# Last attention's keys of five tiles begun while the second layer's pipeline fills, its values while the third layer's pipeline empties

## The chip, the cores and the metric

The kernel runs on one core of a Trainium2 chip. A core has five engines with an instruction stream each: TensorE (PE: matrix products and transposes, into PSUM), VectorE (DVE), ScalarE (ACT), GpSimd (POOL) and SyncE (SP, which issues the DMAs here). Each stream runs in its written order; semaphores make one engine wait for another. The metric is the device time of one execution in microseconds (us), the median of the runs, lower being better.

## The reference

Four layers are applied to x, 16 sequences of 128 tokens with 256 features; a second input, ctx, has the same shape. Each layer is a cross-attention to ctx and a feed-forward part, both with a layer norm ahead and added to x. Cut to what matters, with numpy-like names:

```python
for xattn, ffn in layers:                 # layers 0, 1, 2, 3
    x = x + xattn(layernorm(x), ctx)
    x = x + ffn(layernorm(x))

def L3_xattn(x, cond):                    # the last attention: all tokens of all sequences
    q = x @ Wq + bq                       # 16 heads of 16
    k, v = split(cond @ Wkv + bkv)        # of ctx alone, not of x
    q, k = fake_int8(q, per token and head), fake_int8(k, per token and head)
    v = fake_int8(v, scale over all 2048 tokens)
    p = fake_uint8(softmax(q @ k.T))
    return (p @ v) @ Wp + bp
```

Layers 0 to 2 attend within a sequence, so a tile of 128 tokens passes through them by itself. The last attention has every token attend to all 2048 context tokens, so that all keys and values have to be there before its first tile is done. Its keys and values depend on ctx alone, so they can be worked out at any time before. The scale of the values is a maximum over all tokens: the values are computed once for the maximum and once more to be quantized.

## The kernel before

The work falls into three sections. `l0` does layer 0; `middle` does layers 1 and 2 and, beside them, the keys and values of layer 3; `l3` does layer 3. A tile is one sequence (128 tokens on the partitions); x stays in SBUF in 16 tiles for the whole kernel.

In `middle` each piece of work is a Python generator, and a `yield` ends a step of it. `side_by_side` (L122) takes a table that says at which step each generator starts, and advances all running generators by one step in turn. This gives the order in which instructions are recorded. Outside `l3`, whose order is written out by hand, the framework's scheduler then lays the recorded instructions out on each engine. The table before: tile t begins the second layer's attention (`l1_xattn`) at step 4t, its feed-forward part (`l1_ffn`) at 4t+3, the third layer's attention (`l2_xattn`, eight steps) at 4t+7, its feed-forward part (`l2_ffn`, four steps) at 4t+16, and the last attention's keys of tile t (`l3_keys`, three steps) at 4t+2. The values (`l3_values`, 17 steps) begin at step 4. So a tile enters every four steps; steps 0 to 16 fill the pipeline, and from step 64 on it empties, the last step being 79.

PSUM has eight banks, shared out by tag: e (1 bank: all of `l1_xattn`, and transposes and the last product of `l1_ffn`), w (3: the wide products of both feed-forward parts), x (2: `l2_xattn`), av (1), and f (1: transposes and the last product of `l2_ffn`, and in the version before all of the keys and values). The stream of keys and values, "kv", has one buffer for each SBUF tile that it names.

One piece of values (`piece`, L836) is a product of two 128x512 float32 matmuls into a bank (vT), and an ACT copy with the bias into SBUF (L841). In the first eight steps DVE then takes the maximum (L845). In the later eight, DVE scales and rounds (L853), POOL subtracts the rounding constant into a bfloat16 tile vi (L855), PE transposes its four blocks (vtp, L859), and ACT copies them into `v_int` (L860). One tile of keys is a product of two 128x256 matmuls in a bank (k), its quantization on DVE and POOL (from L773 and L818), a split into three bfloat16 parts on DVE (L824, L826), and eight transposes (htp, L789) with an ACT copy (L790).

What leaves each stage is added to x on DVE: line 608 after `l1_xattn`, 675 after `l1_ffn`, 717 after `l2_xattn`, 770 after `l2_ffn`. In `l2_ffn` the products vecs are followed by a routing on DVE, POOL's z (L764), z's transposes and the product out. When the middle is over, its SBUF is given to the weights of `l3`.

Of the kernel before, what the change touches and what calls it, by code (L numbers as in the profile page):

```python
# [30 lines left out]
NT = 16  # L31
# [9 lines left out]
class Net:  # L41
# [820 lines left out]
    def middle(self, w3):  # L862

        with (self.tc.tile_pool(name="w1", bufs=1) as self.w, self.psum(e=1, w=3, x=2, av=1, f=1)):
            self.tag = "e"
            w1f = self.l1_ffn_weights()
            w2x, w2f, w3k = self.l2_xattn_weights(), self.l2_ffn_weights(), self.l3_kv_weights()
            with (self.stream("f", bufs=1, small=2) as s2f, self.stream("x", bufs=1, small=2) as s2x,
                  self.stream("kv", bufs=1, small=2, tag="f") as s3, self.stream("f1", bufs=1, small=2, tag="e") as s1f,
                  self.stream("x1", bufs=1, small=2, tag="e") as s1x):  # L870
                starts = {}
                for t in range(NT):
                    for step, st, make in ((0, s1x, lambda p, t=t: self.l1_xattn(t, p)),
                                           (3, s1f, lambda p, t=t: self.l1_ffn(t, w1f, p)),
                                           (7, s2x, lambda p, t=t: self.l2_xattn(t, w2x, p)),
                                           (16, s2f, lambda p, t=t: self.l2_ffn(t, w2f, p)),
                                           (2, s3, lambda p, t=t: self.l3_keys(t, w3k, w3, p))):
                        starts.setdefault(4 * t + step, []).append((st, make))
                starts[4].append((s3, lambda p: self.l3_values(w3k, w3, p)))
                self.side_by_side(starts)  # L880
        self.tag, self.small = None, self.small0

# [379 lines left out]
```

## Time and profile before

| what | value |
|---|---|
| median of three runs | 3008.33 us (3003.62 to 3014.27) |
| time of the profiled execution | 3011.51 us |
| span of its instructions | 3009.8 us |
| PE busy | 2460.5 us (82%) |
| DVE busy | 1956.3 us (65%) |
| ACT busy | 1755.0 us (58%) |
| POOL busy | 1000.7 us (33%) |
| first and last exit of line 608 | 1183.3 and 1736.7 us |
| first and last exit of line 770 | 1329.7 and 1862.5 us |

A profile is of one execution; its instants are us from the span's start. A line of a timeline has the start, the duration, the engine, the source line, the operation, the tile written and those read, the shape, the number of instructions merged, and in brackets the idle time of the engine just before it and who ended that. A line of a tile has the smallest, median and largest duration in ns, and the first and last start. A line of waits has the sum, the number and the longest, in us. A float32 matmul shows as two records. The granted clock is the share of full speed that TensorE was allowed.

### The profile page before, as it was taken

Reading aid. Unit: us, or ns where it says so; the run is one execution under the profiler, and the core shown is the slowest. Engines: PE = TensorE matmul, PEld = TensorE weight load, DVE = VectorE, ACT = ScalarE, POOL = GpSimd, SP = SyncE. Lnnn points to the kernel's source line nnn. Section 1 sums busy time; section 2 is a strip of 40 time slices with the busy share of each in tenths; the row PEclk is TensorE's granted clock in tenths of the full one; section 3 lists DMA queues with packets and bytes.
Section 4 is the critical chain, followed back from the end, with each engine's and each line's share of the span. In section 5 each row is a group of like instructions: output and inputs, shape, how many; then the busy total and the mean of one; then the engine's idle time right before and its main releaser. Section 6 shows DMA issues by size and latency. Waiting matters only on the chain. (4 is left out here: it accounts for less than half of the span.)

```text
span 3009.8 us, 41685 instructions
## 1 busy us (share of the span) xinstructions
PE 2460.5 (82%) x14066; PEld 1556.2 (52%) x14066; DVE 1956.3 (65%) x5041; ACT 1755.0 (58%) x4636; POOL 1000.7 (33%) x1587
## 2 busy tenths in 40 slices
PE   4789999999999875888888885777777777777778
PEld 2456666666666543456555653344444444444445
DVE  2455666666665434566666653887788787878784
ACT  1234444444444332555555541998888888888885
POOL 2344444444443322555555541111111111112111
PEclk9899999999999887999999997589899898989999
DMA  5000000000000003000000002876666666666673
GB/s 205 1 1 1 1 1 1 1 1 1 1 1 1 1 28 102 6 3 5 5 5 4 3 1 72 154 135 123 124 117 128 121 124 121 126 122 125 118 128 62
DMA packets 559830, 171.38 MB, mean 57 GB/s; under 512 B 538912, under 2 KB 555904, under 8 KB 558848
## 3 DMA queue, kind: packets, MB, share of 16 engines
q1 hardware_dynamic: 559616, 168.72, 27.8%
q8 instruction: 111, 1.82, 0.2%
q14 instruction: 103, 0.84, 0.1%
HBM read 32.37 MB, written 2.10 MB: 11 GB/s over the span
## 5 line engine op out<-in xcount | busy, mean ns | idle before, releaser
L938 ACT ACTIVATE p<-piece,nb,hs 128x512 int16<-128x512 f32 x1024 | 785.2, 791 | 27.4 <-issue 17.0
L922 DVE TENSOR_REDUCE nm<-piece 128x1 f32<-128x512 f32 x1024 | 652.1, 684 | 107.7 <-PE piece L916 99.8
L916 PE MATMUL piece<-kst,qT 128*128 128x512 bf16 x1024 | 366.5, 414 | 200.6 <-DVE ma L1099 89.6
L1100 POOL TENSOR_TENSOR act<-ma,mb 128x176 f32<-128x176 f32 x160 | 89.0, 558 | 765.1 <-DVE ma L1099 764.7
L233 PE MATMUL gu<-w_L_ffn_wgu,mhT 128*128 128x352 f32 x640 | 252.5, 523 | 11.6 <-ACT p L938 8.0
L225 ACT COPY pT<-tp 128x512 f32<-128x512 f32 (+1 forms) x208 | 116.6, 563 | 201.6 <-PE tp L209 200.1
L916 PEld LDWEIGHTS <-qT 128*128 128x128 bf16 x1024 | 77.4, 99 | 297.2 <-issue 168.8
L938 ACT ACTIVATION_READ_ACCUMULATOR p<-piece,nb,hs 128x1 f32 x1024 | 222.2, 217 | 0.0
L259 POOL TENSOR_TENSOR kx<-kT,hmask 128x512 f32<-128x512 f32 x128 | 132.8, 1043 | 190.4 <-PE scores L262 125.4
L264 DVE TENSOR_REDUCE mx<-scores 128x4 f32<-128x512 f32 x128 | 88.2, 689 | 161.3 <-PE scores L262 161.0
L233 PEld LDWEIGHTS gu<-w_L_ffn_wgu,mhT 128*128 128x128 f32 x640 | 122.7, 205 | 131.4 <-ACT p L938 83.5
L950 PEld LDWEIGHTS <-pT 128*128 128x128 f16 x4096 | 144.7, 99 | 82.6 <-issue 68.0
L278 PEld LDWEIGHTS av<-v,pT 128*128 128x128 f32 x1024 | 136.2, 201 | 78.2 <-ACT pT L225 66.6
L233 PE MATMUL gu<-w_L_ffn_wgu,hT 128*128 128x352 f32 x512 | 173.7, 461 | 2.1 <-DVE act L432 1.6
L524 ACT ACTIVATE s<-s,nb,qs 128x128 f32<-128x128 f32 x256 | 123.2, 482 | 87.2 <-DVE nb L522 87.2
L278 PE MATMUL av<-v,pT 128*128 128x17 f32 x1024 | 136.3, 265 | 41.0 <-ACT pT L225 41.0
L269 ACT ACTIVATE p<-scores,mx,qs 128x128 f32<-128x128 f32 x256 | 96.9, 459 | 118.8 <-DVE mx L267 111.0
L950 PE MATMUL av<-v_int,pT 128*128 128x16 bf16 x4096 | 143.7, 171 | 19.6 <-DVE o L1021 19.6
L262 PE MATMUL scores<-kx,qT 128*128 128x512 f32 x256 | 153.0, 682 | 2.3 <-ACT qT L225 1.8
L539 PE MATMUL oproj<-w_L_ffn_oT,oT 128*128 128x256 f32 x512 | 128.9, 396 | 3.7 <-ACT oT L533 3.6
L1119 PE MATMUL moe<-w_L_ffn_wd,aT 128*128 128x256 f32 x448 | 127.7, 434 | 3.6 <-ACT p L938 3.6
L233 PE MATMUL q<-w_L_ffn_qT,hT 128*128 128x512 f32 x256 | 127.9, 600 | 2.1 <-DVE rot L478 2.0
(362 smaller groups left out, 5305.7 us busy)
## 6 DMA issues: line engine op xcount, KB each, us to landing
pT<-p SPq DMA_TRANSPOSE x256, 4.3
w_L_ffn_wgu<-in_L_ffn_wgu SPq DMA_DIRECT2D x1, 3520.0 KB, 11.6
w_L_ffn_wgu<-in_L_ffn_wgu SPq DMA_DIRECT2D x1, 2816.0 KB, 12.7
x<-in_x SPq DMA_DIRECT2D x16, 128.0 KB, 4.5
ctxT<-in_ctxT SPq DMA_DIRECT2D x4, 512.0 KB, 5.2
w_L_ffn_qT<-in_L_ffn_qT SPq DMA_DIRECT2D x1, 2048.0 KB, 7.9
w_L_ffn_oT<-in_L_ffn_oT SPq DMA_DIRECT2D x1, 2048.0 KB, 15.6
ctx<-in_ctx SPq DMA_DIRECT2D x16, 128.0 KB, 2.0
```

The costliest lines, as they stand in the source:

```text
L225: nc.scalar.copy(out[:, j0:j0 + m, :], ps)
L233: self.nc.tensor.matmul(ps, a, b, start=(j == 0), stop=(j == n - 1))
L259: nc.gpsimd.tensor_tensor(kx, kT[oc].unsqueeze(1).to_broadcast([P, 4, P]), self.hmask[:, hs].unsqueeze(2).to_broadcast([P, 4, P]), ALU.mult)
L262: nc.tensor.matmul(ps, qT[:, oc, :], kx, start=True, stop=True)
L278: nc.tensor.matmul(av[:, 4 * g + h, :], pT[:, h, :], v[:, 4 * g + h, :], start=True, stop=True)
L524: nc.scalar.activation(s[:, j, :], s[:, j, :], AF.Exp, bias=nb[:, j:j + 1], scale=qs[:, j:j + 1], accum_out=z[:, j:j + 1])
L539: nc.tensor.matmul(proj, oT[:, j, :], w["o"][:, c, :], start=(c == 0), stop=(c == 15))
L916: nc.tensor.matmul(ps, qTs[t % 2][:, hd, :], kst[q // 2][:, hd // 2, 512 * (q % 2):512 * (q % 2) + 512], start=True, stop=True)
L922: nc.vector.tensor_reduce(st["nm", u][:, q:q + 1], st["s", u, q][0], AX.X, ALU.max, negate=True)
L938: nc.scalar.activation(p[:, 512 * q:512 * q + 512], ps, AF.Exp, bias=nb, scale=st["sq", t][:, hd:hd + 1], accum_out=st["z", t][:, hd, q:q ...
L950: nc.tensor.matmul(st["av", t][:, hd, :], pb[:, c, :], v[:, c, hd * 16:(hd + 1) * 16], start=(c == 0), stop=(c == NT - 1))
L1119: nc.tensor.matmul(ps, st["aT", k][:r, j, :], wd[:r, c, :], start=(c == 0), stop=(c == 13))
```

## The change

The keys leave the table of the loop over tiles. A loop of its own starts them at step 2t for the first five tiles (0, 2, 4, 6, 8) and at 4t-8 from the sixth on (12, 16, ..., 52). The values begin at step 61 instead of step 4, and take their PSUM from bank e instead of bank f. Keys stay in bank f. No instruction is added or removed.

```diff
-                                           (16, s2f, lambda p, t=t: self.l2_ffn(t, w2f, p)),
-                                           (2, s3, lambda p, t=t: self.l3_keys(t, w3k, w3, p))):
+                                           (16, s2f, lambda p, t=t: self.l2_ffn(t, w2f, p))):
                         starts.setdefault(4 * t + step, []).append((st, make))
-                starts[4].append((s3, lambda p: self.l3_values(w3k, w3, p)))
+
+
+                for t in range(NT):
+                    starts.setdefault(2 * t if t < 5 else 4 * t - 8, []).append((s3, lambda p, t=t: self.l3_keys(t, w3k, w3, p)))
+                starts.setdefault(4 * NT - 3, []).append((s3[:2] + ("e",), lambda p: self.l3_values(w3k, w3, p)))
                 self.side_by_side(starts)
```

## The prediction

> **What bounds the kernel now.** The page's slices first: the middle section, which the change touches, is slices 15 to 24 of the 40.
>
> ```profile
> span 3009.8 us, 41685 instructions
> ...
> PE   4789999999999875888888885777777777777778
> ...
> PEclk9899999999999887999999997589899898989999
> ```
>
> PE is the fullest engine in the middle and no other comes near it. Next, busy time by stage of that section. Columns: stretch, its length, then busy us of PE, PEld, DVE, ACT and POOL, granted clock, DMA share, GB/s.
>
> ```profile
> 1183.00:1330.00 147.00, 117.72 (x510) 69.36 (x510) 86.26 (x257) 74.46 (x175) 80.04 (x123) 0.89 0.02 6
> 1330.00:1745.00 415.00, 357.46 (x1779) 246.50 (x1777) 283.29 (x797) 222.94 (x567) 219.85 (x353) 0.94 0.01 4
> 1745.00:1820.00 75.00, 62.90 (x305) 42.82 (x304) 36.73 (x87) 35.33 (x87) 24.26 (x35) 0.93 0.00 1
> 1820.00:1862.50 42.50, 20.56 (x66) 13.93 (x66) 13.26 (x27) 3.91 (x7) 9.63 (x10) 0.72 0.00 0
> ```
>
> The rows are the fill, the steady part, and the emptying in two pieces. PE is 80% busy in the fill, 86% when the pipeline is full (one tile each 37.5 us), 84% in the first part of the emptying and 48% in its last 42 us. Then the tile that moves, and what its instructions wait for:
>
> ```profile
> L233 PE MATMUL vT<-ctxT,w_L_xattn_Wkv x64: 592/592/1223, 1190.1 to 1314.5; 128*128 128x512 f32 x64
> L841 ACT ACTIVATE vT<-vT,c_L_xattn_bkv x16: 687/688/720, 1196.5 to 1315.5; 128x512 f32<-128x512 f32 x16
> L845 DVE TENSOR_REDUCE vam<-vT x8: 670/680/686, 1197.2 to 1236.6; 128x1 f32<-128x512 f32 x8
> L853 DVE TENSOR_SCALAR vT<-vT,vr x8: 476/486/781, 1243.5 to 1319.4; 128x512 f32<-128x512 f32 x8
> L855 POOL TENSOR_SCALAR vi<-vT x8: 1499/1505/1595, 1244.3 to 1321.2; 128x512 bf16<-128x512 f32 x8
> ...
> PE vtp L859 <- POOL vi L855: 7.5, 5, 3.0
> ```
>
> All values work lies in the fill. Last, the emptying in order of time: where each of the last five tiles leaves (line 770), and PE and POOL around the last two.
>
> ```profile
> 1744.96 0.41 DVE L770 TENSOR_TENSOR x<-out,x 128x256 f32<-128x256 f32 x1
> 1779.47 0.42 DVE L770 TENSOR_TENSOR x<-out,x 128x256 f32<-128x256 f32 x1 [1.04 <-PE out L233]
> 1811.27 0.42 DVE L770 TENSOR_TENSOR x<-out,x 128x256 f32<-128x256 f32 x1 [3.73 <-PE out L233]
> 1838.70 0.42 DVE L770 TENSOR_TENSOR x<-out,x 128x256 f32<-128x256 f32 x1 [12.23 <-PE out L233]
> 1862.54 0.42 DVE L770 TENSOR_TENSOR x<-out,x 128x256 f32<-128x256 f32 x1 [11.83 <-PE out L233]
> ```
>
> ```profile
> 1814.10 3.68 PE L233 MATMUL vecs<-w_L_ffn_AT,hT 128*128 128x512 f32 x8
> ...
> 1829.12 1.12 PE L209 MATMUL tp<-ident,z 128*128 128x128 f32 x4 [9.27 <-POOL z L764]
> ...
> 1839.18 0.44 PE L209 MATMUL tp<-ident,ln_h 128*128 128x128 f32 x2 [0.52 <-DVE x L770]
> ...
> 1852.86 1.12 PE L209 MATMUL tp<-ident,z 128*128 128x128 f32 x4 [9.08 <-POOL z L764]
> ```
>
> ```profile
> 1827.15 1.92 POOL L764 TENSOR_TENSOR z<-routes,v 128x1024 f32<-128x1024 f32 x1
> ```
>
> The end is a chain of third-layer feed-forward tiles, one after the other: the next tile's transposes (1839.18) follow the previous tile's exit (1838.70), since both use the one "f" bank. Only inside it does PE stand idle, about 9 us per tile, while routes and z are made.
>
> **What the change costs, part by part.**
>
> *What moves.* PE: 64 vT records, 35.5 us busy (2.2 us for each of 16 pieces), and 32 vtp transposes, 3.7 us: 39.2 us. ACT: 16 x 0.69 and eight copies of 0.60 us; DVE: 8 x 0.68 and 8 x 0.49; POOL: 8 x 1.5. Keys cost PE 1.7 us a tile (halves of 0.5 us and eight transposes of some 0.08). They issue no DMA; SP's order is the same in both programs, and so is PE's up to the first tile's qv transposes (1188.8 us). So nothing changes before 1188.8, nor in the last layer, whose weights start to load when the middle ends (1862 us).
>
> *The fill.* Starts of line 608 (first tiles out of the second layer's attention) are 1183.3, 1214.2, 1243.1, 1275.3, 1320.6 and 1361.3: gaps of 30.9, 28.9, 32.2, 45.3 and 40.7, together 178.0 us, with PE busy 142.3. Taking out 39.2 and adding 3.4 (two keys more than before by then) leaves 106.5. Were PE as full as in the steady part (86%), that is 124 us, a gain of 54; at the first gap's 65% (20.24 of 30.9) it is 164, a gain of 14. Between these ends I go gap by gap. In the first, what values add on the tile's own chain can be read off the timeline: 1.3 us of vT ahead of the gate matmul, 1.2 on ACT and DVE ahead of "a", some 0.6, 0.7 and 0.7 later: 4.5, so 26.4 without values, and 3 more for two extra keys (DVE waited 3.3 us for POOL's k there): 29.5. The next three then take 28, 27 and 28, by the same chain; the fifth, in which the third layer's feed-forward joins, 35. Sum 147.5: **30 us less** (14 to 54).
>
> The Trainium skill speaks against this. "TensorE: Matmul & The Clock Gate", section "HAM oscillation — how this bites in real kernels", says that gaps of PE over about 3.4 us drop its clock to half. Row first: the gap of 1183.3 to 1214.2 was granted 0.83 at 65% busy. By the row the thinner fill stays near 0.8, and I count 2 us of it within the 28s. By the rule, were the first three gaps at 0.5, their 47 us of PE work (70.9 busy, less 27.3 of values, plus two keys), now at a mean clock of 0.87, would be 82 us in a chain of 84.5: it would be PE-bound at about 95, and the gain 19. I take the row, as fresh matmuls come every few us from two layers.
>
> *The steady part.* Same work a tile (32 us of PE per 37.5), another order: keys now stand beside the third layer's feed-forward. PE's stalls per tile in the trace are about 5.5 us, most of it av waiting for ACT's pT (2.1, 0.7 and 0.3 us). In the new order one such pair has the ten out matmuls between its halves, one has q and k, one z, and one nothing; aT's second half lost the o transposes that covered it. I count zero, with 0.5 us either way per tile for eleven tiles: -6 to +6.
>
> *The emptying.* By the new order, the exits above have 5.5 pieces between the first two, then 4 pieces and 3 vtp groups, then 3.5 and 4, then 1 and 1. In turn:
> 1744.96 to 1779.47: 12 us of vT. Three vT matmuls stand between p's transposes and av, where PE waited anyhow (8.8 us of stalls in 1722 to 1779). Count +11.
> To 1811.27: 8.8 + 1.4 = 10 us, against 5.5 us of old stalls; but vtp stands soon after its piece, and a piece needs ACT 0.69 + DVE 0.49 + POOL 1.5 and hand-overs, 3.4 us, before it: count +6.
> To 1838.70: the skill's rule weighs here. The row: POOL was idle, and z began at 1827.15, 9.4 us after vecs ended. "PSUM — Partial Sum Buffer", section "Engine vs sequencer instructions", says that GpSimd's queue is strict first in, first out; the new order has four vi ahead of this z. By the row z is no later. By the rule, walked by hand from the previous exit (PE rows as above): vecs end at 11.9, the 14th piece's vT at 15.1, its vi at 18.4, routes' v at 21: z is not held, but vtp of the 14th holds PE 2.5 us and the next vtp, whose vi stands behind z, holds the out matmuls 1 us. Exit after 31.5, not 27.4: +4; by the row alone +2. I take +4.
> To 1862.54: two vT before the transposes (+1.7), and the last vtp inside vecs waits for its vi (+2): +3.5.
> Sum **+24.5** (10, were the idle 22 us of PE in the last 42.5 used well, to 45: the slower rival below). Two pieces stand ahead of the first of these exits, where two keys and then an htp are gone: 4.4 us of PE against 4.0, so nothing.
>
> Sum: -30 + 0 + 24.5 = -5.5 us. The profiled execution took 3011.5 us around its span of 3009.8, 3 us over the runs' median, which I shift: 3008.3 - 5.5 = **3003 us**.
>
> **The rivals.**
> *A larger gain.* PE idles 22 us in the last 42.5, and vT fills waits behind pT: emptying costs 10, total -20 or better: about 2988. For it: 48% busy at the end. Against: only 1 to 4.5 pieces stand there in the order.
> *Slower: PE in order behind vtp.* Each vtp waits for vi at the head of PE's queue, with single buffers for vT and vi and the single "e" bank, which the second layer's last feed-forward tile wants too. The fill's waits were 7.5 us in five cases, while much else ran. If every piece is paid in full, 39.2 us and 8 x 1.5 of waits, less what is hidden at the end (6), emptying costs 45: +15, or 3023. It decides once emptying costs more than the fill gains, 30 us, or 1.9 us for each of 16 pieces that hold PE 2.45.
> *Slower: the steady order.* One us more on each of eleven tiles is 3014; two, 3025. Against: the work is the same, PE 86% busy.
> *It does little.* The fill is bound by its chain, gains 18 (the clock rule's 19), and emptying costs 20 to 24: 3010 to 3014.
>
> **How the numbers follow.** My forecast (2992 to 3014) gets 0.42; the larger gain 0.22; vtp 0.24; the steady order 0.08; little 0.04. A change under 0.3%, 9 us, can't be told from none in this kernel. Faster: 0.22 and 0.16 of my own case, 0.38. Slower: 0.24 + 0.08 = 0.32. Same: the other 0.26 of my case and 0.04, 0.30. The range reaches to the larger gain and to both slower cases: 2974 to 3028.
>
> **What would show it.** The gaps of line 608 in the fill should be near 29, 28, 27, 28 and 35, the third layer's first tile should leave (line 770) near 1306, not 1329.7, the steady gap should be 37.5, and the last four exits should be 45, 38, 31 and 27 us apart. Wrong if the steady gap is not within 0.5 of 37.5, if the first gaps stay at 31 (clock near 0.5), or if PE's waits for vi pass 15 us.

## The result

The changed kernel takes **3083.96 us** (median of 4 runs, 3081.62 to 3085.16) against 3006.93 for the one before (4 runs on the same chip): ratio 1.0251, 95% interval 1.0233 to 1.0268. It is 77 us slower, far outside the range of 2974 to 3028. The profiled spans are 3082.7 and 3009.8 us, a difference of 72.9. The page of the changed kernel, its span and slices:

```profile
span 3082.7 us, 41713 instructions
...
PE   4789999999998874778777896677777777777778
...
PEclk9999999999999986798888898668999999899999
```

In the steady part of the middle PE's digits fell from 8 to 7 (with one 8) and the clock's from 9 to 8; where the fill begins PE shows a 4, and the clock a 6 and a 7. Next, rows with the same columns as those shown of before: the fill, the steady part (here one tile shorter, to the 11th exit of line 770), then its last tile with the first two gaps of the emptying, and the last two gaps.

```profile
1181.80:1325.60 143.80, 100.34 (x446) 65.25 (x451) 89.85 (x255) 66.05 (x159) 74.64 (x124) 0.78 0.02 6
1325.60:1759.00 433.40, 343.16 (x1591) 239.68 (x1600) 242.52 (x717) 203.11 (x509) 201.36 (x319) 0.86 0.01 4
1759.00:1876.20 117.20, 103.03 (x450) 65.17 (x451) 59.34 (x148) 56.67 (x138) 43.82 (x60) 0.94 0.00 1
1876.20:1936.70 60.50, 41.54 (x159) 25.80 (x157) 18.85 (x44) 14.63 (x28) 17.27 (x15) 0.83 0.00 1
```

PE is busy 17 us less in the fill, and the fill is hardly shorter: the clock went from 0.89 to 0.78. The steady part was granted 0.86 instead of 0.94, and PE is busy 79% of it instead of 86%. The values have moved where the diff says, at the durations they had:

```profile
L233 PE MATMUL vT<-ctxT,w_L_xattn_Wkv x64: 592/593/1220, 1773.4 to 1910.1; 128*128 128x512 f32 x64
...
PE vtp L859 <- POOL vi L855: 11.2, 6, 3.3
```

And the last five exits of line 770:

```profile
1794.31 0.42 DVE L770 TENSOR_TENSOR x<-out,x 128x256 f32<-128x256 f32 x1 [2.64 <-PE out L233]
1834.38 0.42 DVE L770 TENSOR_TENSOR x<-out,x 128x256 f32<-128x256 f32 x1 [1.97 <-PE out L233]
1876.25 0.42 DVE L770 TENSOR_TENSOR x<-out,x 128x256 f32<-128x256 f32 x1 [8.79 <-PE out L233]
1909.06 0.42 DVE L770 TENSOR_TENSOR x<-out,x 128x256 f32<-128x256 f32 x1 [8.60 <-PE out L233]
1936.68 0.42 DVE L770 TENSOR_TENSOR x<-out,x 128x256 f32<-128x256 f32 x1 [12.67 <-PE out L233]
```

Layer 0, which is the same in both programs, ends with its last exit of line 554, before, then after:

```profile
1154.63 0.42 DVE L554 TENSOR_TENSOR x<-moe,x 128x256 f32<-128x256 f32 x1 [5.11 <-PE moe L233]
1151.14 0.42 DVE L554 TENSOR_TENSOR x<-moe,x 128x256 f32<-128x256 f32 x1 [5.11 <-PE moe L233]
```

The sum from there on by exits of line 770, in us:

| stage | before | after | difference | predicted |
|---|---|---|---|---|
| layer 0's last exit | 1154.63 | 1151.14 | -3.5 | 0 |
| from there to the first exit | 175.04 | 174.48 | -0.6 | -24 |
| first to 12th exit | 415.3 | 468.7 | **+53.4** | -6 |
| 12th to 16th exit | 117.6 | 142.4 | +24.8 | +24.5 |
| the rest of the span | 1147.3 | 1146.0 | -1.3 | 0 |

The -30 of the fill was counted over five gaps of line 608, and so stands in two rows: -24 up to the first exit (forecast near 1306), and -6 behind it. The 3.5 us of layer 0 differ from one profiled execution to the next and are no gain of the change; they are about as much as the spans' difference (72.9) falls short of that of the medians (77.0). Two terms of the prediction failed, the steady part by 53 us and the fill by some 25. The emptying came out as summed up.

**Where the steady part's time goes.** In the full pipeline the gap of line 608 is 44.3 us, not 37.5. The timeline of the changed kernel shows, in every tile, one stretch like this (start, duration, engine, line, ..., idle time before it and its releaser):

```profile
1553.59 1.27 POOL L657 TENSOR_TENSOR a<-a,r_L_ffn_subln_weight 128x512 f32<-128x512 f32 x1
...
1554.82 0.62 POOL L781 TENSOR_TENSOR k<-k,hr 128x256 f32<-128x256 f32 x1
1555.53 0.88 POOL L782 TENSOR_SCALAR k<-k 128x256 f32<-128x256 f32 x1
1556.49 0.85 POOL L818 TENSOR_SCALAR k<-k 128x256 f32<-128x256 f32 x1
1557.42 0.62 POOL L820 TENSOR_TENSOR k<-k,hs 128x256 f32<-128x256 f32 x1
1558.00 1.04 POOL L259 TENSOR_TENSOR kx<-kT,hmask 128x512 f32<-128x512 f32 x1
1559.00 1.26 POOL L657 TENSOR_TENSOR a<-a,r_L_ffn_subln_weight 128x512 f32<-128x512 f32 x1
1560.29 1.22 DVE L664 TENSOR_REDUCE am<-a 128x1 f32<-128x1024 f32 x1 [3.87 <-POOL a L657]
1561.43 0.22 DVE L267 TENSOR_SCALAR mx<-mx,qs 128x4 f32<-128x4 f32 x1
1561.74 1.50 ACT L269 ACTIVATE p<-scores,mx,qs 128x128 f32<-128x128 f32 x4 [4.12 <-DVE mx L267]
1563.12 0.60 ACT L225 COPY pT<-tp 128x512 f32<-128x512 f32 x1
1563.77 1.89 PE L278 MATMUL av<-v,pT 128*128 128x17 f32 x8 [5.91 <-ACT pT L225]
```

The second half of line 657 had its input at 1554.1 (line 654's second half on DVE started at 1553.38 and took 0.75), but stands in POOL's queue behind the keys' four operations and a kx (259, the third layer's masked keys; it stands there in the kernel before too). So the second layer's maximum (664) starts 4 us late. The third layer's mx (267, the scaled maximum of its scores) stands behind that maximum in DVE's queue, p (269, the exponentials) behind mx, a ready copy of pT (225, an earlier p transposed) behind p in ACT's queue, and av (278, the product with the values) behind that copy in PE's. Four queues pass on one late step, and PE stands idle for 5.9 us; in the kernel before, the same wait is 2.1 us. There both halves of 657 precede the keys' operations. What follows on PE is in slices of 4 us of the same tile (columns as above, the granted clock third from the end):

```profile
1555.30:1559.30 4.00, 2.56 (x12) 1.37 (x10) 1.12 (x3) 0.95 (x3) 3.75 (x6) 1.00 0.00 0
1559.30:1563.30 4.00, 0.00 (x0) 0.00 (x0) 3.01 (x11) 1.56 (x5) 2.18 (x5) 0.89 0.00 0
1563.30:1567.30 4.00, 2.82 (x12) 2.42 (x12) 4.00 (x19) 1.58 (x4) 0.76 (x2) 0.50 0.03 6
1567.30:1571.30 4.00, 3.38 (x18) 2.65 (x19) 0.81 (x3) 0.71 (x2) 0.00 (x0) 0.50 0.00 0
```

After the stall the clock is 0.50 for some 10 us (from 1562.5 to 1572.6), and the matmuls there take nearly twice as long: the eight of av 1.89 us, against 1.06 in the kernel before. The mean clock of 0.85 in these tiles, if the rest ran at 1.00, stands for some 13 us of each tile at half speed.

### The profile page after: what moved, and what is told of

Its sections match the earlier page's. It is cut to its first block, busy times and chain, and to the rows that moved or that the text cites. A ratio compares the mean times of both kernels' runs of the same rounds, so it can differ in the third digit from the quotient of the medians.

```text
span 3082.7 us, 41713 instructions
## 1 busy us (share of the span) xinstructions
PE 2486.7 (81%) x14049; PEld 1576.3 (51%) x14066; DVE 1947.6 (63%) x5041; ACT 1757.4 (57%) x4636; POOL 1003.5 (33%) x1587
## 5 line engine op out<-in xcount | busy, mean ns | idle before, releaser
L278 PEld LDWEIGHTS av<-v,pT 128*128 128x128 f32 x1024 | 143.6, 211 | 89.7 <-ACT pT L225 80.8
```

What stands on the lines that cost most here:

```text
L278: nc.tensor.matmul(av[:, 4 * g + h, :], pT[:, h, :], v[:, 4 * g + h, :], start=True, stop=True)
```

## The experiments

All numbers of the steady part come from one place: the window between line 608's 8th and 14th exits, divided by six tiles. PE's work per tile in it is the same in all the kernels.

| kernel | gap | PE busy | PE idle | clock | median, us |
|---|---|---|---|---|---|
| before | 37.5 | 32.1 | 5.4 | 0.95 | (3005 to 3011) |
| after | 44.3 | 35.0 | 9.3 | 0.85 | 3083.96 |
| e1 values alone | 37.5 | 32.1 | 5.4 | 0.95 | 3027.42 |
| e2 keys alone | 44.3 | 35.0 | 9.3 | 0.85 | 3083.87 |
| e3 keys at 4t-7 | 42.3 | 34.2 | 8.1 | 0.87 | 3055.62 |
| e4 after, 657 on DVE | 40.7 | 33.5 | 7.2 | 0.91 | 3048.17 |
| f1 keys early, old step of four | 37.5 | 32.1 | 5.4 | 0.95 | 3011.51 |
| f2 before, 657 on DVE | 37.65 | 31.9 | 5.8 | 0.95 | 3004.78 |
| f4 before, POOL delayed | 40.0 | 32.9 | 7.1 | 0.93 | 3046.18 |
| g3 after, keys off POOL | 40.1 | 33.5 | 6.6 | 0.89 | 3039.95 |
| g4 before, keys off POOL | **36.4** | 31.9 | 4.5 | 0.95 | **2995.59** |
| h1 g4, keys at 4t+1 | 40.9 | 34.4 | 6.5 | 0.87 | 3031.19 |
| h2 g4, keys at 4t+3 | 37.55 | 31.7 | 5.9 | 0.95 | 3008.42 |

### Which half of the change: e1 and e2

e1 takes the values' half alone; the keys start at 4t+2 as before:

```diff
-starts.setdefault(2 * t if t < 5 else 4 * t - 8, []).append((s3, ...l3_keys...))
+starts.setdefault(4 * t + 2, []).append((s3, ...l3_keys...))
```

> Values moved to the emptying as in the change, keys left at step 4t+2 as before. Theory A (the keys' four POOL operations stand in POOL's queue ahead of the second half of the norm-weight product of line 657, so that DVE's maximum of line 664 and, behind it, the attention's scaled maximum of line 267 wait some 4 us a tile): steady gap of line 608 back at 37.5 us; emptying as in the changed kernel, +25; fill gains 5 to 25; total 3007 to 3027. Theory B (the fill and steady part are slower because TensorE, without the values, is less busy and gets a lower clock): steady gap stays near 44, total near 3080.

e2 takes the keys' half alone:

```diff
-starts.setdefault(4 * NT - 3, []).append((s3[:2] + ("e",), ...l3_values...))
+starts[4].append((s3, ...l3_values...))
```

> Keys moved as in the change, values left in the fill and in bank f as before. Theory A: steady gap 44, so +53 over eleven tiles and nothing in the emptying; the fill holds both values and the early keys, +0 to +15; total 3055 to 3080. Theory B: with the values back in the fill nothing is lost but by the order of the fill, steady gap 37.5, total 3005 to 3015.

Measured: e1 3027.42, ratio 1.0065 (1.0040 to 1.0091), steady gap 37.5, emptying 140.8 us (+23.2). The first exit of line 770 is 7.0 us earlier than before, but layer 0 ended 4.8 us earlier in this execution: the fill is 2.2 us shorter. e2 3083.87, ratio 1.0242 (1.0216 to 1.0268), steady gap 44.3, fill 16.8 us longer counted from layer 0's last exit, emptying 121.5. Theory A had the gaps right; its total for e2 was 4 us too low. So the keys' new place alone makes the whole loss in the steady part, with the same 5.9 us stall of av; the values' move alone costs 23 at the end and returns 2 in the fill.

### Why the keys cost 6.8 us a tile: e3, e4, f1, f2, f4

The changed kernel starts the keys at a multiple of four steps, one started before at 4t+2. e3 starts them at 4t-7 (values late), f1 at 4t-6, the old place in the cycle of four but two tiles ahead (values early):

```diff
-2 * t if t < 5 else 4 * t - 8
+2 * t if t < 5 else 4 * t - 7      # e3; f1 has 4 * t - 6
```

> As the changed kernel, but from the sixth tile on keys start one step later (4t-7, so 13, 17, ...). By the built order the keys' POOL operations then stand behind the second half of line 657, as before the change; DVE's line 664 still stands ahead of line 267, as in the changed kernel; and the keys' htp falls into the step in which the third layer's feed-forward part takes bank f three times. Theory A: the 3.9 us wait of DVE for line 657 falls below 1.5, steady gap 38 to 39.5, total 3020 to 3040. Theory C (the keys now meet the third layer's feed-forward part in bank f): steady gap 43 or more, total 3070 or more.

> Values as before; keys of the first five tiles at 2t as in the change, the others at 4t-6 (14, 18, ...), so early too, but in the same place of the four-step cycle as before. Theory A (what costs is the place in POOL's and DVE's queues, not that keys come early): steady gap 37.5; the fill a little longer than before by the extra keys, 0 to +8; total 3000 to 3018. If early keys themselves cost (theory D), the total is near 3060 or more.

Measured: f1 3011.51, ratio 1.0023 (1.0014 to 1.0031), gap 37.5. Doing keys two tiles early costs 0.2%, 6 us of the median. In the profiled execution, the slowest of 13 at 3021.90, the first exit of line 770 comes 16 us later, as keys and values now share the fill, and 5 us of it are back by the 12th exit. In the steady part it costs nothing; there the step in the cycle is what costs. e3, 3055.62 (ratio 1.0149, 1.0123 to 1.0174), lies between the two theories: the gap is 42.3 in this window and 40.8 in most tiles. Its keys follow 657 in POOL's queue, line 664 waits only 1.6 us a tile, and still the gap is 3 us or more too long. So POOL's delay couldn't be all of it.

e4 takes the changed kernel with line 657 on DVE, so that nothing of POOL stands ahead of the maximum; f2 makes the same edit in the kernel before, and is the control:

```diff
-nc.gpsimd.tensor_tensor(a[:, n:n + 512], a[:, n:n + 512], w["subln"][:, n:n + 512], ALU.mult)
+nc.vector.tensor_tensor(a[:, n:n + 512], a[:, n:n + 512], w["subln"][:, n:n + 512], ALU.mult)
```

> The changed kernel with the norm-weight product of line 657 on DVE instead of POOL: what the keys' POOL operations stand ahead of is no longer on POOL, at a price of two DVE operations of some 0.7 us a tile. Theory A: DVE's maximum no longer waits for POOL, steady gap 38 to 40, total 3020 to 3045. Theories B and C: steady gap stays at 44, total near 3084.

> The kernel before with the norm-weight product of line 657 on DVE: what that edit costs or brings by itself, to set against the run in which it was made on the changed kernel (3048, steady gap about 40.2). Theory A: the 2.7 us a tile that were left there are its own price, so the steady gap is near 40 here too, total 3030 to 3040. If instead the keys' new place still costs by another way, the steady gap here is 37 to 38.5, total 3000 to 3020.

Measured: e4 3048.17, ratio 1.0131 (1.0107 to 1.0154); f2 3004.78, ratio 1.0002 (0.9993 to 1.0012). The edit by itself is worth nothing, and in the changed kernel it takes 44.3 to 40.7: **3.6 us a tile are the late half of 657**. Another 3.1 (40.7 against 37.65) stay, which is more than theory A allowed (a gap of 38 to 40).

f4 does the opposite: in the kernel before, POOL does two more operations on an unread scratch tile (nothing is left out) between the halves of 657:

```diff
+            if j == 0:
+                wait = pool.tile([P, 512], BF16, name="wait", tag="wait")
+                for _ in range(2):
+                    nc.gpsimd.tensor_scalar(wait, a[:, n:n + 512], 1.0, None, ALU.add)
```

> The kernel before, with two POOL operations of 1.5 us on a scratch tile behind the first half of line 657, so that its second half, and DVE's line 664, come about 3 us later, as behind the keys' four operations. In this order DVE's line 267 stands ahead of line 664. Theory A1 (a delay of POOL at that point is enough): steady gap 41 or more, total 3045 or more. Theory A2 (it costs only where line 664 stands ahead of line 267 and so holds up the attention): steady gap 37.5 to 39.5, total 3008 to 3030.

Measured: 3046.18, ratio 1.0131 (1.0114 to 1.0148), gap 40.0. DVE's maximum (line 664 is 668 here) now waits some 3 us for line 657 in every tile. A delay of 3.0 us on POOL, an engine that is busy 58% of the time here, lengthens the tile by 2.5 us in the window (3.1 in most tiles), between the gaps of the two theories. It is enough by itself; mx need not stand behind the maximum for that, since here it stands ahead of it. The chain goes another way through the same four queues: the softmax of the second layer's attention (598, nm in line 600, s in line 601) stands behind the maximum on DVE, and the pT copy behind its exponential on ACT.

```profile
1519.68 1.22 DVE L668 TENSOR_REDUCE am<-a 128x1 f32<-128x1024 f32 x1 [2.97 <-POOL a L657]
1521.45 0.40 ACT L601 ACTIVATE s<-s,nm 128x128 f32<-128x128 f32 x1 [2.77 <-DVE nm L600]
1522.47 1.89 PE L278 MATMUL av<-v,pT 128*128 128x17 f32 x8 [4.03 <-ACT pT L225]
```

### The other half: g3, g4, h1, h2

g3 and g4 leave 657 on POOL and take the keys' four operations off it, in the changed kernel and in the kernel before (a fifth, the clearing of parts in line 822, stays on POOL):

```diff
-nc.gpsimd.tensor_tensor(v, v, r.unsqueeze(2).to_broadcast([P, NH, 16]), ALU.mult)
-nc.gpsimd.tensor_scalar(src, src, MAGIC, None, ALU.add)
+nc.vector.tensor_tensor(v, v, r.unsqueeze(2).to_broadcast([P, NH, 16]), ALU.mult)
+nc.vector.tensor_scalar(src, src, MAGIC, None, ALU.add)
...
-nc.gpsimd.tensor_scalar(k, k, -MAGIC, None, ALU.add)
-nc.gpsimd.tensor_tensor(kh, kh, sk.unsqueeze(2).to_broadcast([P, NH, 16]), ALU.mult)
+nc.vector.tensor_scalar(k, k, -MAGIC, None, ALU.add)
+nc.vector.tensor_tensor(kh, kh, sk.unsqueeze(2).to_broadcast([P, NH, 16]), ALU.mult)
```

> The changed kernel with the keys' four POOL operations (lines 781, 782, 818, 820) done by DVE instead; the order of the rest stays that of the changed kernel, the maximum of line 664 still ahead of mx of line 267 in DVE's queue. Theory A: all of the 6.8 us a tile comes from POOL handing over the second half of line 657 late. Then with POOL free of the keys the steady gap falls to within 1 us of that of g4 (37.5 to 38.5), DVE no longer waits for line 657, and the median is 3025 to 3038 (before, with -4 for the fill and +24 for the emptying). Theory B: the keys' place beside the third layer's feed-forward costs some 2.6 us a tile by itself, as the 40.2 us with line 657 on DVE suggest (there ln_r of a layer norm stood in POOL's queue behind a wait for sq_junk). Then the gap is 40 or more and the median 3048 or more.

> The kernel before with the keys' four POOL operations done by DVE: the control for g3. POOL and DVE both have room, so the edit by itself should be worth little: steady gap 37.0 to 38.2, median 3000 to 3013. A gap above 39 would say that these operations cost on DVE, and g3 would have to be read against that.

Measured: g3 3039.95, ratio 1.0111 (1.0085 to 1.0137), gap 40.1; g4 **2995.59, ratio 0.9955 (0.9937 to 0.9973)**, gap 36.4. DVE's wait for 657 is down to 0.5 us a tile in g3, from 3.9, and 3.7 us a tile over its control remain: the second way to about the same remainder, so theory A fell. (Theory B had the gap right and the median too high, as the control itself is faster.) The control was a surprise: it beats both kernels, by 15 us of the median before in its batch.

h1 and h2 start from g4 and move only the keys, by one step to either side:

```diff
-(2, s3, lambda p, t=t: self.l3_keys(t, w3k, w3, p))
+(1, s3, lambda p, t=t: self.l3_keys(t, w3k, w3, p))      # h1; h2 has 3
```

> The kernel before, the keys' POOL operations on DVE (g4: steady gap 36.5 us, 2995.6), and the keys of tile t begun at step 4t+1 instead of 4t+2; the values as before. Theory P: it is the changed kernel's place, the same step as the second half of line 657 (4t), that breaks up the order on PE and costs some 2.5 to 4 us a tile besides POOL's delay; the step next to the old one costs little. Then the gap is 36 to 38 and the median 2990 to 3013. Theory Q: before's place was the only good one, and every other costs 2 us a tile or more: gap above 38.5, median above 3018.

> As the run at step 4t+1, but the keys of tile t begun at step 4t+3, on the other side of the old place. Theory P: gap 36 to 38, median 2990 to 3013. Theory Q: gap above 38.5, median above 3018. The values stay early and the tile order of the rest is before's.

Measured: h1 3031.19, ratio 1.0092 (1.0065 to 1.0120), gap 40.9; h2 3008.42, ratio 1.0003 (0.9990 to 1.0017), gap 37.55. Neither theory holds as put: one neighbour costs 4.5 us a tile, the other 1.1. (DVE waits for 657 in both, 1.1 us in every tile of h2 and 1.6 in every other tile of h1, so that this wait can't be what sets them apart.) What h1 has in common with the other slow orders is in PE's waits, 1450 to 1612 us; first h1, then the same wait in g4:

```profile
PE tp L209 <- ACT aT L215: 3.5, 4, 0.9
PE down L233 <- ACT aT L215: 3.1, 4, 0.8
```

```profile
PE tp L209 <- ACT aT L215: 0.4, 2, 0.2
```

aT is the second layer's `a`, transposed in two halves; ACT copies each half out of PSUM, and the product "down" takes both. The order of PE at that point in before, then in after (o is what the third layer's attention gives):

```profile
1536.96 0.63 PE L209 MATMUL tp<-ident,a 128*128 128x128 f32 x4
1538.00 0.44 PE L209 MATMUL tp<-ident,o 128*128 128x128 f32 x2 [0.41 <-DVE o L291]
1538.46 1.00 PE L209 MATMUL tp<-ident,a 128*128 128x128 f32 x4
```

```profile
1567.46 1.09 PE L209 MATMUL tp<-ident,a 128*128 128x128 f32 x4 [0.87 <-ACT aT L215]
...
1569.33 1.86 PE L233 MATMUL down<-tern,aT 128*128 128x256 bf16 x8 [0.46 <-ACT aT L215]
...
1571.20 0.63 PE L209 MATMUL tp<-ident,o 128*128 128x128 f32 x2
```

In before, g4 and h2 the o transposes stand between the two halves of a, and the third layer's out product and one scores product between the second half and down; they cover ACT's copies of aT. In after, g3, h1, e3 and e4 they stand behind all or half of the down product, and there PE waits at both copies: in the six tiles of the table 1.65 us a tile in h1, e3 and g3, 1.3 in after, 1.2 in e4, and at most 0.2 in all the other kernels. The idle time and the slower clock together are the remainder: from g4 to h1 idle grows by 2.0 us a tile and PE's busy time, for the same work, by 2.5. That the aT waits are the main part of this idle time is read from the waits; no run put the o transposes back by themselves. In after and e3 a second wait grows, for z, to 1.8 us a tile from 0.6 in before: there a kx, late for want of its scores, stands ahead of z in POOL's queue and holds it for 1.1 to 1.4 us. The keys' sharing of bank f with `l2_ffn` (theory C) shows in none of these windows: no wait of PE ends on the copy of the keys' transposes (line 790).

### The fill and the emptying: f3 and g5

f3 is e1 with ten unread products (two 128x512 matmuls each, nothing left out) in the place where values were, to keep PE busy in the fill:

```diff
+                starts[4].append((s3, lambda p: self.warm(w3k, 10)))
...
+    def warm(self, w, n):
+        for j in range(n):
+            ps = self.mm([P, 512], "warm")
+            self.matmul_acc(ps, [(w["kv"][:, c, D:D + P], self.ctxT[:, c, 0:512]) for c in range(2)])
+            yield
```

> Values alone moved to the emptying (3027 before), and in the fill ten pairs of matmuls as large as a values piece, from step 4 on, whose product nobody reads: the values' load on TensorE without their work on ACT, DVE and POOL. Theory E (without values the fill runs at a lower TensorE clock and so gains little): granted clock in the first two gaps back at 0.8 or more (0.60 and 0.76 without them), the gaps 28 to 31 instead of 34.6 and 32.6, total 3018 to 3024. Theory F (the fill's chain is held by the keys and the order of the queues, not by the clock): gaps stay at 33 or more, total 3027 to 3035.

Measured: 3018.40, ratio 1.0043 (1.0027 to 1.0060). The middle ends 9.3 us earlier than in e1 (1868.6 against 1877.9), with more work in it and though layer 0 ended 4.3 us later. The first three gaps of line 608 in e1, then in f3:

```profile
1179.70:1214.30 34.60, 15.23 (x58) 9.31 (x59) 16.06 (x53) 8.75 (x17) 13.94 (x24) 0.60 0.04 9
1214.30:1246.90 32.60, 25.08 (x96) 14.65 (x98) 19.02 (x56) 16.62 (x43) 17.16 (x28) 0.76 0.01 1
1246.90:1278.50 31.60, 24.01 (x110) 15.64 (x109) 16.67 (x47) 15.89 (x40) 13.41 (x24) 0.78 0.02 5
```

```profile
1183.50:1212.50 29.00, 20.03 (x79) 10.18 (x81) 13.96 (x47) 8.67 (x17) 11.53 (x21) 0.83 0.03 7
1212.50:1240.30 27.80, 21.65 (x93) 11.78 (x92) 16.23 (x50) 14.61 (x38) 16.18 (x26) 1.00 0.02 6
1240.30:1275.10 34.80, 27.49 (x142) 17.65 (x142) 21.14 (x61) 18.14 (x46) 18.39 (x32) 0.90 0.02 5
```

With PE kept warm the first five gaps take 161.3 us instead of 173.9 (178.0 before): in these two executions the clock took some 12 us of the fill's gain, as theory E had it. At the first exit of line 770 f3 is 5.9 us ahead of e1, and 10.2 counted from layer 0's last exit. The direction is surer than the size: the medians differ by 9.0 us, by 4.2 when each is set against the runs of the kernel before beside it, and f3's profiled execution (3012.04) is the fastest of its four.

g5 is e1 with the values in bank f instead of e:

```diff
-starts.setdefault(4 * NT - 3, []).append((s3[:2] + ("e",), ...l3_values...))
+starts.setdefault(4 * NT - 3, []).append((s3, ...l3_values...))
```

> Keys as before, values late, as in the run with values alone (3027, emptying 140.8 us from line 770's 12th to 16th exit), but the values in bank f, which the third layer's feed-forward tiles use one after the other, instead of bank e. If the two vT products of a step and the vtp groups hold up the tiles by their PSUM bank, the emptying gets longer by 5 us or more (146 or longer, median 3032 or more). If only PE's time and order count, as the prediction summed it up, it stays at 138 to 144 and the median at 3024 to 3031.

Measured: 3034.28, ratio 1.0094 (1.0069 to 1.0119), emptying 149.0 us against e1's 140.8, steady gap 37.5. Bank e is worth 8 us in the traces and 7 in the medians (the intervals of the two ratios overlap): the pieces hold up the last tiles also by the bank.

## Why the prediction was wrong

*The steady part, "I count zero, with 0.5 us either way per tile": the step that failed.* It was +53.4 us between the first and the 12th exit, 6.8 a tile where the pipeline is full. The sum asked only for PE's order and its av pairs. It did not follow the keys on POOL, although the rule it cited from the Trainium skill ("PSUM — Partial Sum Buffer", section "Engine vs sequencer instructions": GpSimd's queue is strict first in, first out) is what decides here. The rule was weighed for z in the emptying, where z of the tile that left at 1909.06 was held by DVE's v, with POOL free for 1.5 us before it; it should have been asked of every POOL step that the keys pass, and line 657 was one. The row agrees with the rule: 657's second half, ready at 1554.1, ran at 1559.0. This late half is 3.6 of the 6.8 us (e4), and a like delay alone gives 2.5 (f4).

The other 3.1 to 3.7 us a tile (e4, g3) are nearer to what the prediction named: "aT's second half lost the o transposes that covered it". The loss was seen and then counted at zero. PE's waits there are 1.2 to 1.65 us a tile; the rest of this part is other waits, that for z among them, and the clock. Which of them would go if the o transposes stood in their old place stays open, as does why the keys' step moves these transposes.

*The clock was missing from that step.* PE's busy time per tile went from 32.1 to 35.0 for the same instructions. Of the 6.8 us, 3.9 are idle time and 2.9 slower matmuls. So the added idle time cost about 1.7 times its length.

*The fill, -30: came to -5.1 over the same five gaps, and to nearly nothing at the first exit of line 770.* Gaps of 29.5, 28, 27, 28 and 35 were forecast; 31.7, 38.8, 30.5, 33.5 and 38.4 came. "I take the row, as fresh matmuls come every few us" was wrong, and the clock rule of the Trainium skill ("TensorE: Matmul & The Clock Gate", section "HAM oscillation — how this bites in real kernels") was right in direction: the first two gaps were granted 0.65 and 0.69, not 0.8. Its own estimate of a gain of 19 was still too good. Counted from layer 0's last exit, values alone made the fill 2.2 us shorter (e1), and 12.4 with PE kept warm (f3); the keys' new place gave back 1.6 of e1's gain (after), and beside the values it costs 16.8 (e2). The chain was read too short as well: with PE warm the third to fifth gaps still took 34.8, 32.3 and 37.4, and the first took 29.0 where the forecast, without the 3 us for extra keys that f3 doesn't have, was 26.4 (but f3's extra matmuls stand in that gap too). What else holds the fill is open. POOL is a part of it: with the keys' four operations off POOL the fill is 10.1 us shorter in the changed order (g3, at granted clocks as low as 0.62 and 0.74 in the first two gaps) and 8.4 in the old one (g4).

*The emptying, +24.5: right.* +24.8, and 23.2 with the values alone. By exits: 45, 38, 31 and 27 forecast, 40.1, 41.9, 32.8 and 27.6 measured; the first gap was put 5 us too long and the second 4 too short, so that the sum fits better than its terms, which is in part luck. PE's waits for vi were 11.2 us, under the 15 named as a limit; the rival in which vtp holds PE for 45 us did not come.

*The rivals.* "Slower: the steady order" had the right place, chance 0.08, and 1 to 2 us a tile. "The work is the same" was its counter-argument; the work was, the order of four queues and the clock were not.

## What to carry to other kernels

Before moving a step of low priority, list its instructions on every in-order engine and see what stands directly behind each in the new order, and who waits for that: 4 us on a half-idle engine went through four queues and made a 2.1 us stall of the full one 5.9 us long. Look also at what the moved step's neighbours lose: work that stood between a transpose and its product was cover. Where PE is the bound, count a stall together with the slower clock behind it, and move small operations to an engine that nobody waits for: taking the keys' four operations off POOL, in their old place, is the version that beat both kernels.

## What the runs showed of the hardware

The granted clock in slices of 4 us is mostly 1.00 or 0.50, with mixtures where it changes inside a slice, which agrees with the two states that the Trainium skill states ("TensorE: Matmul & The Clock Gate", section "What's actually happening"). The length of the longest idle gap of PE does not order the kernels, though: f4, with one gap of 4.0 us a tile, was granted 0.93, and g3, with none above 1.75 us, 0.89, while before, with gaps of 2.1, had 0.95. g3's timeline in slices shows the fall behind a thin stretch, without a long gap:

```profile
1532.20:1536.20 4.00, 2.67 (x18) 1.96 (x16) 3.50 (x12) 2.29 (x6) 2.36 (x6) 0.97 0.00 0
1536.20:1540.20 4.00, 2.04 (x8) 1.56 (x9) 4.00 (x22) 1.59 (x5) 1.03 (x2) 0.50 0.02 4
1540.20:1544.20 4.00, 3.22 (x18) 2.56 (x17) 1.71 (x5) 1.06 (x2) 0.00 (x0) 0.50 0.00 0
1544.20:1548.20 4.00, 3.98 (x15) 2.50 (x14) 2.96 (x5) 1.12 (x2) 1.18 (x2) 0.75 0.00 0
```

In 1532 to 1536 PE was 67% busy, and the clock was at half for the next 10 us. The same page has this form as a second one (section "A second HAM failure mode: psum-queue depth-cycling": frequent short idle times between groups of matmuls). What share of which stretch decides is open: g4 had one slice at 48% and kept 1.00.
